# Mamba blocks in a four-layer kernel: the residual added by TensorE, softplus's correction on ScalarE and GpSimd, the layer norm's affine folded into weights

## The chip, the cores and the metric

The kernel runs on one core of a Trainium2 chip. The metric is the device time of one execution in microseconds, the median of several runs. All arithmetic is fp32.

## The reference, cut to what matters

Four layers follow each other on a tensor of 4 images, 96 channels, 64 x 64 pixels. Layers 0 and 2 are two Mamba blocks with a fusion and a batch norm, layer 1 is another state-space layer (ssd), layer 3 a ConvNeXt block. The change touches layers 0 and 2 only. One Mamba block, with L = 4096 positions, C = 96, DIN = 192, 16 states:

```python
mu = seq.mean(-1, keepdims=True)
var = ((seq - mu) ** 2).mean(-1, keepdims=True)
h = (seq - mu) * jax.lax.rsqrt(var + EPS) * ln_g + ln_b
xz = h @ in_w
xs, z = jnp.split(xz, 2, axis=-1)
xp = jnp.pad(xs, ((0, 0), (DCONV - 1, 0), (0, 0)))
xc = sum((conv_w[:, k] * xp[:, k:k + L, :] for k in range(DCONV))) + conv_b
xc = jax.nn.silu(xc)
dbl = xc @ xproj_w                      # dt, B, C
delta = jax.nn.softplus(dt @ dt_w + dt_b)
dA = jnp.exp(delta[..., None] * A)
dBx = delta[..., None] * Bm[:, :, None, :] * xc[..., None]
hstates = jax.lax.associative_scan(comb, (dA, dBx), axis=1)[1]
y = jnp.einsum('blds,bls->bld', hstates, Cm) + Dp * xc
y = y * jax.nn.silu(z)
return y @ out_w                        # and: seq = seq + this
```

## The kernel before, in words

**Stages.** `program` runs `mamba_fusion`, `ssd`, `mamba_fusion`, `convnext` one after the other. A Mamba stage keeps the whole sequence X of the four images in SBUF (96 partitions). It walks over 32 steps: 2 pairs of images, 2 blocks, 8 chunks of T = 512 positions. With two images of 192 channels a step has 384 channel rows, held as three tiles of 128 rows (j = 0, 1, 2).

**A step's two halves.** `mamba_front` prepares a step: layer norm (matmuls with `center` and `mean`, rsqrt on ScalarE), the input projection and the convolution as matmuls with tap-wise weights that already hold the convolution's factors (`wt["conv"]`), Silu, the projection to dt, B and C, softplus, and the products du = delta * xc. It is a generator; each `yield` is a place where the other half may go on. `Scan.run` walks over 24 groups of a step (3 tiles j, 4 quarters q, 2 halves). A group covers two times 128 rows, each 8 channels by 16 states, and 512 positions. The code of `run` issues, for group n: loads of delta rows four groups ahead, `decay` (the exponentials) two ahead, `spread` one ahead, the scan, `sums` two behind, `close` and `project` three and four behind, and as many pieces of the next step's `mamba_front` as the list `PACE` says.

**Who does what in a group.** Delta is written to DRAM (`dd`) and comes back by DMA spread over the states (`da`, a pool of 6 buffers). In three of four groups TensorE spreads du into PSUM (`bs`, L313, two buffers), VectorE multiplies it by B (L335), ScalarE turns da into decays in place (L107). In each fourth group (`dma`) ScalarE writes the decays into that PSUM tile (bs<-da), du comes by DMA (`dg`), and GpSimd multiplies by B (L308). VectorE scans (two instructions, L340), GpSimd multiplies the states by C (hc, L342; 3 buffers), ScalarE saves the last column (L345), TensorE sums over the states (py, L361). When a tile j is done, VectorE gates it (L369), TensorE projects it (po, L377), and VectorE adds it to X (L381).

**Softplus** is worked out as max(x, 0) + ln(1 + u) plus a correction, u = exp(-|x|): Abs, Exp, Ln on ScalarE, the maximum and first sum on VectorE (L267), w = u + 1 on ScalarE written over x in PSUM (L268), u - (w - 1) on VectorE (L270), the sum on GpSimd (L271), and then du (L248).

**Order.** A framework puts in the semaphores and also reorders: instructions are placed per engine by priority and readiness, so the order on an engine isn't quite that of the code. Each engine then works through its own order. The tile pools set how far one engine can be ahead: a tile name or tag with one buffer has to be read out before it is written again. `ua` and `lg` have one buffer each in the kernel before, PSUM's `mm` tag two.

**Activation tables.** Exp and Ln are wanted from one combined table set; `Tables` loads it once and again after each Silu or Gelu (L119), and keeps the exponentials behind a load by a dependency. If an instruction needs a function that the loaded set lacks, the build puts a load ahead of it; such a load carries the line of that instruction (L107).

Of the kernel before, what the change touches and what calls it, by code (L numbers as in the profile page):

```python
# [18 lines left out]
F32 = mybir.dt.float32  # L19
AF = mybir.ActivationFunctionType  # L20
ALU = mybir.AluOpType
# [4 lines left out]
B, C, HH, WW = 4, 96, 64, 64  # L26
L = HH * WW
P = 128
T = 512
# [6 lines left out]
DIN = 192  # L36
# [40 lines left out]
class Consts:  # L77
    def __init__(self, tc, pool):
        nc = tc.nc
        self.act = Tables(tc)  # L80
        self.norms = [pool.tile([C, 2], F32, name=f"bn{i}") for i in range(2)]
        self.ident = pool.tile([P, P], F32, name="ident")
        make_identity(nc, self.ident)

        self.center = pool.tile([C, C], F32, name="center")
        nc.vector.tensor_scalar(self.center, self.ident[:C, :C], -1.0 / C, None, ALU.add)
        self.mean = pool.tile([C, C], F32, name="mean")
        nc.vector.memset(self.mean, 1.0 / C)
        self.eps = pool.tile([P, 1], F32, name="eps")
        nc.vector.memset(self.eps, EPS)  # L90


class Tables:
# [29 lines left out]
def rsqrt(act, out, in_, eps):  # L123

    act.exp_ln(out, in_, AF.Ln, bias=eps)
    act.exp_ln(out, out, AF.Exp, scale=-0.5)
# [28 lines left out]
def mamba_front(tc, k, X, pools, wt, pair, c, h, made):  # L155

    nc = tc.nc  # L160
    work, psum, dram = pools
    if c == 0:
        nc.vector.memset(h[:C, :, 0:3], 0.0)
    else:
        nc.scalar.copy(h[:C, :, 0:3], h[:C, :, T : T + 3])

    def bank(name):
        return psum.tile([P, T], F32, tag="mm", name=name)

    for b in range(2):  # L170
        pc = bank("pc")[:C]
        nc.tensor.matmul(
            pc, lhsT=k.center, rhs=X[:, 2 * pair + b, ds(c * T, T)], start=True, stop=True
        )
        sq = work.tile([P, T], F32, tag="ua", name="sq")[:C]
        nc.scalar.activation(sq, pc, AF.Square)
        yield
        pv = bank("pv")[:C]
        nc.tensor.matmul(pv, lhsT=k.mean, rhs=sq, start=True, stop=True)
        rs = work.tile([P, T], F32, tag="lg", name="rs")[:C]  # L180
        rsqrt(k.act, rs, pv, k.eps[:C])
        yield
        dst = h[:C, b, 3 : 3 + T]
        nc.vector.tensor_tensor(dst, pc, rs, ALU.mult)
        nc.gpsimd.tensor_scalar(dst, dst, wt["ln"][:, 0:1], wt["ln"][:, 1:2], ALU.mult, ALU.add)


    xz = made["xz"] = work.tile([P, 6, T], F32, name="xz", bufs=2)
    for j in range(3):
        pu = bank("pu")  # L190
        for tap in range(4):
            kk = C + 1 if tap == 3 else C
            for r0, r1, d0, d1, b in SEGS[j]:
                nc.tensor.matmul(  # L194
                    pu[r0:r1], lhsT=wt["conv"][:kk, tap, d0:d1], rhs=h[:kk, b, ds(tap, T)],
                    start=(tap == 0), stop=(tap == 3),
                )
            yield
        nc.scalar.copy(xz[:, j], pu)
    k.act.other(xz[:, :3], xz[:, :3], AF.Silu)  # L200
    for j in range(3):
        pz = bank("pz")
        for r0, r1, d0, d1, b in SEGS[j]:
            nc.tensor.matmul(
                pz[r0:r1], lhsT=wt["in"][:, DIN + d0 : DIN + d1], rhs=h[:C, b, 3 : 3 + T],
                start=True, stop=True,
            )
        yield
        nc.scalar.copy(xz[:, 3 + j], pz)


    dbl = work.tile([P, T], F32, name="dbl")
    pd = bank("pd")
    for n in range(2):
        for b in range(2):
            j, r0, r1 = ROWS[b][n if b == 0 else 1 - n]
            nc.tensor.matmul(
                pd[2 * QUART * b : 2 * QUART * (b + 1)], lhsT=wt["xproj"][r0:r1, j],
                rhs=xz[r0:r1, j], start=(n == 0), stop=(n == 1),
            )  # L220
    yield
    nc.scalar.activation(dbl, pd, AF.Identity, bias=wt["one"])


    rows = dram.tile([P, T], F32, name="rows")
    nc.sync.dma_start(rows, dbl)
    bc = made["bc"] = work.tile([P, 2, 2, T], F32, name="bc", bufs=2)


    du = made["du"] = work.tile([P, 3, T], F32, name="du", bufs=2)  # L230
    for j in range(3):
        pt = bank("pt")
        for r0, r1, d0, d1, b in SEGS[j]:
            half = ds(HALFP * b, HALFP)
            nc.tensor.matmul(
                pt[r0:r1], lhsT=wt["dt"][half, d0:d1], rhs=dbl[half], start=True, stop=True,
            )
        delta = work.tile([P, T], F32, name="delta", bufs=2)
        softplus(nc, k.act, work, delta, pt)
        yield  # L240
        if j == 0:
            for b in range(2):
                for q in range(2):
                    r = HALFP * b + (QUART if q else RANK + 1)
                    nc.sync.dma_start(
                        bc[:, b, q], rows[r : r + NST, None].to_broadcast([NST, HEIGHT, T])
                    )
        nc.gpsimd.tensor_tensor(du[:, j], delta, xz[:, j], ALU.mult)  # L248
        for name, x in (("dd", delta), ("dg", du[:, j])):
            made[name, j] = dram.tile([P, T], F32, name=f"{name}{j}")  # L250
            nc.sync.dma_start(made[name, j], x)
    k.act.other(xz[:, 3:], xz[:, 3:], AF.Silu)
# [4 lines left out]
LEAD = 4  # L257


def softplus(nc, act, work, out, x):  # L260

    u = work.tile([P, T], F32, tag="ua", name="ua")
    t = work.tile([P, T], F32, tag="lg", name="lg")
    nc.scalar.activation(u, x, AF.Abs)
    act.exp_ln(u, u, AF.Exp, scale=-1.0)
    act.exp_ln(t, u, AF.Ln, bias=1.0)
    nc.vector.scalar_tensor_tensor(out, x, 0.0, t, ALU.max, ALU.add)  # L267
    nc.scalar.activation(x, u, AF.Identity, bias=1.0)  # L268

    nc.vector.scalar_tensor_tensor(t, x, 1.0, u, ALU.subtract, ALU.subtract, reverse1=True)  # L270
    nc.gpsimd.tensor_tensor(out, out, t, ALU.add)  # L271


class Scan:
# [96 lines left out]
    def project(self, g, b):  # L371

        nc = self.tc.nc
        xz, wt = g["made"]["xz"], g["wt"]
        po = self.psum.tile([P, T], F32, tag="po", name="po", bufs=1)[:C]
        for n, (j, r0, r1) in enumerate(ROWS[b]):
            nc.tensor.matmul(  # L377
                po, lhsT=wt["out"][r0:r1, j], rhs=xz[r0:r1, j], start=(n == 0), stop=(n == 1)
            )
        xs = self.X[:, 2 * g["pair"] + b, ds(g["c"] * T, T)]  # L380
        nc.vector.tensor_tensor(xs, xs, po, ALU.add)  # L381

    def run(self, steps, wts, front, first):

# [35 lines left out]
                next(ahead, None)  # L420


def mamba_weights(nc, act, ident, wpool, w, sub, one7):
    wt = {"one": one7}

    def load(name, shape):
        wt[name] = wpool.tile(shape, F32, name=f"w_{name}{sub}")
        nc.sync.dma_start(wt[name], w[name][sub])

    load("ln", [C, 2])  # L430
    load("in", [C, 2 * DIN])
    conv = wt["conv"] = wpool.tile([C + 1, 4, DIN], F32, name=f"w_conv{sub}")
    nc.sync.dma_start(conv[:C], w["conv_wT"][sub].partition_broadcast(C))
    nc.sync.dma_start(conv[C : C + 1, 3], w["conv_b"][sub : sub + 1])
    nc.vector.tensor_tensor(
        conv[:C], conv[:C], wt["in"][:, None, :DIN].to_broadcast([C, 4, DIN]), ALU.mult
    )
    xp = wt["xproj"] = wpool.tile([P, 3, 2 * QUART], F32, name=f"w_xproj{sub}")
    nc.vector.memset(xp, 0.0)
    nb = RANK + 1 + NST  # L440
# [26 lines left out]
def mamba_fusion(ctx: ExitStack, tc, k, src, dst, w):  # L467

    nc = tc.nc
    one = ctx.enter_context(tc.tile_pool(name="m1", bufs=1))  # L470
# [3 lines left out]
    work = ctx.enter_context(tc.tile_pool(name="mwork", bufs=1))  # L474
    state = ctx.enter_context(tc.tile_pool(name="mstate", bufs=3))
    psum = ctx.enter_context(tc.tile_pool(name="mps", bufs=2, space=PSUM))
    dram = ctx.enter_context(tc.tile_pool(name="mdram", bufs=3, space=DRAM))

    one7 = one.tile([P, 1], F32, name="one7")
    nc.gpsimd.memset(one7, 0.0)  # L480
    for q in range(0, P // QUART, 2):
        nc.gpsimd.affine_select(
            out=one7, in_=one7, compare_op=ALU.not_equal, fill=1.0, base=-(QUART * q + RANK),
            pattern=[[0, 1]], channel_multiplier=1,
        )
    h = one.tile([C + 1, 2, T + 3], F32, name="h")
# [8 lines left out]
    for b in range(2):  # L495
        nc.gpsimd.affine_select(
            out=sel["du"], in_=sel["du"], compare_op=ALU.not_equal, fill=1.0, base=-HALFP * b,
# [14 lines left out]
        nc.vector.bn_stats(stats[:, b * NT + c], xs)  # L512
        nc.sync.dma_start(dst[b, :, ds(c * T, T)], xs)

    wts = [mamba_weights(nc, k.act, k.ident, one, w, 0, one7)]
    carry = one.tile([P, 3, P // HEIGHT], F32, name="carry")
    steps = [(pair, sub, c) for pair in range(B // 2) for sub in range(2) for c in range(NT)]

# [10 lines left out]
    for n, _ in enumerate(front(0, made)):  # L529
        if n % 4 == 3 and n // 4 - 1 in range(B):  # L530
            b = n // 4 - 1
            nc.vector.reduce_sum(gsum[:, b : b + 1], X[:, b], axis=AX.X)
    wts.append(mamba_weights(nc, k.act, k.ident, one, w, 1, one7))

    gpw = one.tile([C, C], F32, name="gpw")
    nc.sync.dma_start(gpw, w["gp_wT"])
# [752 lines left out]
```

## Time and profile before

The median of three runs is 10016.03 us (10013.18 to 10017.02). The profiled execution has a span of 10008.9 us.

| stretch | us | TensorE | VectorE | ScalarE | GpSimd | clock | DMA share |
|---|---|---|---|---|---|---|---|
| Mamba 1, 500 to 592 us | 92 | 81.79 | 86.16 | 57.15 | 78.97 | 0.94 | 0.73 |
| Mamba 1, 1500 to 1592 us | 92 | 82.25 | 86.44 | 56.59 | 79.57 | 0.96 | 0.74 |
| ssd, 3060 to 6260 us | 3200 | 2759.58 | 2088.13 | 1538.09 | 1692.26 | 0.94 | 0.26 |
| Mamba 2, 7000 to 8000 us | 1000 | 871.57 | 935.20 | 625.66 | 852.01 | 0.96 | 0.73 |
| ConvNeXt, 9400 to 10008 us | 608 | 521.13 | 484.68 | 262.57 | 174.93 | 0.90 | 0.34 |

The columns are microseconds of busy time in the stretch; the clock is what TensorE was granted, as a share of full speed. In a line of the groups the columns are: source line, engine, operation, output <- inputs, shapes and count, then busy us, mean ns of one, and after the bar the idle time ahead of them with what ended most of it. A line of the waits gives who waited for whom, us in total, times, and the longest. A line of the timeline gives start us, duration us, engine, line, operation, and in brackets an idle time ahead of it. DVE is VectorE, ACT ScalarE, POOL GpSimd, PE TensorE.

### The profile page before, as it was taken

To read this page: it belongs to the slowest core of one execution; us is meant where nothing else is said; L and a number is where in the kernel's file an instruction comes from. 1 tells how busy PE (TensorE), PEld (TensorE's weight loads), DVE (VectorE), ACT (ScalarE), POOL (GpSimd) and SP (SyncE) were. 2 spreads that over 40 slices of the span, in tenths; PEclk is the share of its full clock that TensorE was granted. 3 is DMA by queue.
4 is the path that set the end of the run, shared out by engine and by line. 5 is a ranking of instruction groups with operands and counts; after the bars stand their busy time and mean duration, and the time that the engine had idled before them with its cause. 6 is when DMAs were issued, how large, how long until landed. Compare 5 with 4: busy or idle time off the path is not lost. (4 is left out here: it accounts for less than half of the span.)

```text
span 10008.9 us, 110272 instructions
## 1 busy us (share of the span) xinstructions
PE 8562.4 (86%) x33120; PEld 3566.0 (36%) x33120; DVE 8200.6 (82%) x10877; ACT 5497.9 (55%) x10460; POOL 6966.5 (70%) x4600
## 2 busy tenths in 40 slices
PE   7888888888886888888888888788888888887688
PEld 1222212222214766666776676122222222221122
DVE  7999999999994666667666666799999999999787
ACT  5566666656653445445445444566666665665244
POOL 6888888888883555555555555688888888888322
PEclk9999999999997999999999999899999999999798
DMA  7777777777773223223222221777777767777442
GB/s 190 200 205 204 201 206 207 201 201 209 204 197 105 72 66 94 65 66 95 72 66 74 81 64 51 188 201 204 210 200 203 208 196 204 207 204 199 113 99 73
DMA packets 802257, 1527.53 MB, mean 153 GB/s; under 512 B 123933, under 2 KB 127161, under 8 KB 800890
## 3 DMA queue, kind: packets, MB, share of 16 engines
q1 hardware_dynamic: 801658, 1520.47, 54.6%
q8 instruction: 263, 4.31, 0.2%
q14 instruction: 336, 2.75, 0.1%
HBM read 1229.30 MB, written 155.98 MB: 138 GB/s over the span
## 5 line engine op out<-in xcount | busy, mean ns | idle before, releaser
L342 POOL TENSOR_TENSOR hc<-hs,bc 128x1024 f32<-128x1024 f32 x1536 | 3608.0, 2355 | 622.2 <-DVE hs L340 554.8
L340 DVE TENSOR_TENSOR_SCAN hs<-da,carry,bs 128x512 f32<-128x512 f32 x2016 | 2466.4, 1264 | 79.2 <-POOL du L308 1.0
L107 ACT ACTIVATE da<-da,w_a 128x512 f32<-128x512 f32 x2304 | 1616.5, 716 | 1268.5 <-DMA da<-dd 1218.7
L361 PE MATMUL py<-hc,selsum 128*32 128x512 f32 x6144 | 1801.4, 638 | 462.5 <-POOL hc L342 448.3
L313 PE MATMUL bs<-du,seldu 64*128 64x512 f32 x4608 | 1573.3, 676 | 204.2 <-DVE hs L340 194.5
L335 DVE TENSOR_TENSOR bs<-bs,bc 128x1024 f32<-128x1024 f32 x1152 | 1397.7, 1213 | 184.0 <-PE bs L313 181.6
L308 POOL TENSOR_TENSOR du<-du,bc 128x1024 f32<-128x1024 f32 x384 | 904.5, 2355 | 281.3 <-DMA du<-dg 160.5
L863 POOL TENSOR_TENSOR seg<-seg,cb 128x384 f32<-128x384 f32 x512 | 514.7, 1006 | 818.1 <-DVE cb L862 750.0
L361 PEld LDWEIGHTS py<-hc,selsum 128*32 128x32 f32 x6144 | 240.6, 110 | 1815.1 <-POOL hc L342 1118.2
L313 PEld LDWEIGHTS bs<-du,seldu 64*128 64x128 f32 x4608 | 446.0, 195 | 1196.2 <-DVE hs L340 852.1
L848 DVE TENSOR_SCALAR seg<-dr,dac 128x128 f32<-128x128 f32 x1536 | 660.4, 458 | 256.9 <-PE y L892 249.3
L194 PE MATMUL pu<-h,w_conv 96*128 96x512 f32 (+3 forms) x2048 | 834.6, 629 | 6.5 <-ACT rs L107 6.3
L340 DVE TENSOR_TENSOR_SCAN hs<-bs,carry,du 128x512 f32<-128x512 f32 x672 | 823.5, 1260 | 7.8 <-issue 5.0
L799 PE MATMUL front<-pk,sconv 128*128 128x512 f32 x1536 | 767.9, 609 | 9.2 <-ACT z L787 5.1
L915 ACT ACTIVATE y<-yz 128x192 f32<-128x192 f32 x512 | 186.0, 363 | 919.3 <-DVE yz L914 918.3
L867 POOL TENSOR_TENSOR xs<-pre,coef 128x576 f32<-128x576 f32 x512 | 598.3, 1175 | 56.2 <-ACT pre L112 31.5
L810 PE MATMUL front<-sconv,pk 128*128 128x192 f32 x3072 | 577.2, 330 | 45.3 <-DVE pre L815 36.0
L1152 DVE SCALAR_TENSOR_TENSOR acc<-pad,c_conv,acc 96x1024 f32<-96x1024 f32 x336 | 491.9, 1468 | 109.1 <-ACT acc L1143 58.0
L902 POOL TENSOR_TENSOR y<-y,xs 128x192 f32<-128x192 f32 x496 | 293.5, 592 | 412.8 <-DVE y L901 412.1
L345 ACT COPY carry<-hs 128x2 f32<-128x2 f32 x1344 | 250.7, 187 | 564.2 <-DVE hs L340 560.4
L107 ACT ACTIVATE bs<-da,w_a 128x512 f32<-128x512 f32 x768 | 522.0, 680 | 2.5 <-DMA da<-dd 0.7
L810 PEld LDWEIGHTS front<-sconv,pk 128*128 128x128 f32 x3072 | 497.4, 191 | 69.3 <-DVE pre L815 57.7
(191 smaller groups left out, 13881.2 us busy)
## 6 DMA issues: line engine op xcount, KB each, us to landing
da<-dd SPq DMA_DIRECT2D x3072, 256.0 KB
du<-dg SPq DMA_DIRECT2D x768, 256.0 KB
dr<-rows SPq DMA_DIRECT2D x256, 384.0 KB
bc<-rows SPq DMA_DIRECT2D x256, 256.0 KB
dd<-delta SPq DMA_DIRECT2D x192, 256.0 KB
dg<-du SPq DMA_DIRECT2D x192, 256.0 KB
pk<-xn SPq DMA_DIRECT2D x128, 384.0 KB
pk<-xn SPq DMA_DIRECT2D x128, 256.0 KB
```

The costliest lines, as they stand in the source:

```text
L107: self.last = self.scalar.activation(out, in_, func, **kw)
L194: nc.tensor.matmul(pu[r0:r1], lhsT=wt["conv"][:kk, tap, d0:d1], rhs=h[:kk, b, ds(tap, T)], start=(tap == 0), stop=(tap == 3),)
L308: nc.gpsimd.tensor_tensor(g["du"], g["du"], self.b_or_c(g, 0), ALU.mult)
L313: nc.tensor.matmul(g["bs"][:, i], lhsT=self.sel["du"][rows, g["half"], g["q"]], rhs=g["made"]["du"][rows, g["j"]], start=True, stop=True,)
L335: nc.vector.tensor_tensor(dbx, dbx, self.b_or_c(g, 0), ALU.mult)
L340: nc.vector.tensor_tensor_scan(hs[:, i], da[:, i], dbx[:, i], init, ALU.mult, ALU.add)
L342: nc.gpsimd.tensor_tensor(g["hc"], hs, self.b_or_c(g, 1), ALU.mult)
L361: nc.tensor.matmul(py[rows], lhsT=self.sel["sum"][:, g["q"]], rhs=g["hc"][:, i], start=(g["q"] == 0), stop=(g["q"] == NQU - 1),)
L799: nc.tensor.matmul(p, lhsT=self.conv[:, i, DI + q * DST : DI + (q + 1) * DST], rhs=pk[:, i, ds(c * T, T)], start=(i == 0), stop=(i == 2),)
L810: nc.tensor.matmul(p, lhsT=pk[:, i, ds(c * Q, Q)], rhs=self.conv[:, i, :DI], start=(i == 0), stop=(i == 2),)
L848: nc.vector.tensor_scalar(seg[:, h], g["pair"]["dr"][:, c % 2 * NH + h], made["dac"][:, n0 + h : n0 + h + 1], 0.0, ALU.subtract, ALU.min,)
L867: nc.gpsimd.tensor_tensor(xs, x.to_broadcast([P, 3, NH, HD]), coef.to_broadcast([P, 3, NH, HD]), ALU.mult)
```

## The change

It has three parts, all in the Mamba stages. The residual: TensorE adds X into the projection's PSUM by a matmul with the identity, and ScalarE copies the sum back to X, in place of VectorE's addition. Softplus: the correction is worked out by two ScalarE instructions (u + 1, then - 1, with a bias tile `minus`) and a GpSimd subtraction, in place of ScalarE's one and VectorE's one; ScalarE writes to `lg` and no longer to PSUM, and `ua` and `lg` get two buffers. Layer norm: its gain is multiplied into the weights of convolution and z, its shift becomes one more weight row against a row of ones in h, made at the start by small matmuls (`shift`), so that GpSimd's affine on h falls away. What it is for: to take work off VectorE, and the affine off GpSimd.

```diff
@@ mamba_front
-        nc.vector.memset(h[:C, :, 0:3], 0.0)
+        nc.vector.memset(h[:, :, 0:3], 0.0)
     else:
-        nc.scalar.copy(h[:C, :, 0:3], h[:C, :, T : T + 3])
+        nc.scalar.copy(h[:, :, 0:3], h[:, :, T : T + 3])
...
-        sq = work.tile([P, T], F32, tag="ua", name="sq")[:C]
+        sq = work.tile([P, T], F32, tag="ua", name="sq", bufs=2)[:C]
...
-        rs = work.tile([P, T], F32, tag="lg", name="rs")[:C]
+        rs = work.tile([P, T], F32, tag="lg", name="rs", bufs=2)[:C]
         rsqrt(k.act, rs, pv, k.eps[:C])
         yield
-        dst = h[:C, b, 3 : 3 + T]
-        nc.vector.tensor_tensor(dst, pc, rs, ALU.mult)
-        nc.gpsimd.tensor_scalar(dst, dst, wt["ln"][:, 0:1], wt["ln"][:, 1:2], ALU.mult, ALU.add)
+        nc.vector.tensor_tensor(h[:C, b, 3 : 3 + T], pc, rs, ALU.mult)
...
-                    pu[r0:r1], lhsT=wt["conv"][:kk, tap, d0:d1], rhs=h[:kk, b, ds(tap, T)],
+                    pu[r0:r1], lhsT=wt["conv"][:, tap, d0:d1], rhs=h[:, b, ds(tap, T)],
...
-                pz[r0:r1], lhsT=wt["in"][:, DIN + d0 : DIN + d1], rhs=h[:C, b, 3 : 3 + T],
+                pz[r0:r1], lhsT=wt["z"][:, d0:d1], rhs=h[:, b, 3 : 3 + T],
@@ softplus
-    u = work.tile([P, T], F32, tag="ua", name="ua")
-    t = work.tile([P, T], F32, tag="lg", name="lg")
+    u = work.tile([P, T], F32, tag="ua", name="ua", bufs=2)
+    t = work.tile([P, T], F32, tag="lg", name="lg", bufs=2)
     nc.scalar.activation(u, x, AF.Abs)
     act.exp_ln(u, u, AF.Exp, scale=-1.0)
     act.exp_ln(t, u, AF.Ln, bias=1.0)
     nc.vector.scalar_tensor_tensor(out, x, 0.0, t, ALU.max, ALU.add)
-    nc.scalar.activation(x, u, AF.Identity, bias=1.0)
-
-    nc.vector.scalar_tensor_tensor(t, x, 1.0, u, ALU.subtract, ALU.subtract, reverse1=True)
-    nc.gpsimd.tensor_tensor(out, out, t, ALU.add)
+
+    nc.scalar.activation(t, u, AF.Identity, bias=1.0)
+    nc.scalar.activation(t, t, AF.Identity, bias=minus)
+    nc.gpsimd.tensor_tensor(u, u, t, ALU.subtract)
+    nc.gpsimd.tensor_tensor(out, out, u, ALU.add)
@@ Scan.project
+        xs = self.X[:, 2 * g["pair"] + b, ds(g["c"] * T, T)]
+        nc.tensor.matmul(po, lhsT=self.k.ident[:C, :C], rhs=xs, start=True, stop=False)
         for n, (j, r0, r1) in enumerate(ROWS[b]):
             nc.tensor.matmul(
-                po, lhsT=wt["out"][r0:r1, j], rhs=xz[r0:r1, j], start=(n == 0), stop=(n == 1)
-            )
-        xs = self.X[:, 2 * g["pair"] + b, ds(g["c"] * T, T)]
-        nc.vector.tensor_tensor(xs, xs, po, ALU.add)
+                po, lhsT=wt["out"][r0:r1, j], rhs=xz[r0:r1, j], start=False, stop=(n == 1)
+            )
+        nc.scalar.copy(xs, po)
@@ mamba_weights
+    shift = wpool.tile([C, C + 1], F32, name="w_shift")
+    nc.vector.memset(shift, 0.0)
+    nc.vector.tensor_copy(shift[:, C:], wt["ln"][:, 1:2])
+    for n in range(0, 5, 2):
+        m = min(2, 5 - n)
+        ps = psum.tile([P, T], F32, tag="mm", name="ps")[: C + 1, : m * DIN]
+        nc.tensor.matmul(ps, lhsT=shift, rhs=both[:C, n : n + m], start=True, stop=True)
+        nc.scalar.copy(both[C:, n : n + m].rearrange("p k n -> p (k n)"), ps[C:])
+    nc.vector.tensor_tensor(conv[C:, 3], conv[C:, 3], wx[C:], ALU.add)
+    nc.vector.tensor_scalar_mul(both[:C], both[:C], wt["ln"][:, 0:1])
```

## The prediction, made before the changed kernel ran

> **What bounds the kernel now.** I read the page first (busy shares, 40 slices), then the waits of VectorE, then one Mamba step on each engine in order of time. The page's slices show four stretches: VectorE is nine tenths busy in the two Mamba stages (to about 3050 us, and about 6250 to 9330 us); the rest is not touched by the change.
>
> ```profile
> PE 8562.4 (86%) x33120; PEld 3566.0 (36%) x33120; DVE 8200.6 (82%) x10877; ACT 5497.9 (55%) x10460; POOL 6966.5 (70%) x4600
> L342 POOL TENSOR_TENSOR hc<-hs,bc 128x1024 f32<-128x1024 f32 x1536 | 3608.0, 2355 | 622.2 <-DVE hs L340 554.8
> L340 DVE TENSOR_TENSOR_SCAN hs<-da,carry,bs 128x512 f32<-128x512 f32 x2016 | 2466.4, 1264 | 79.2 <-POOL du L308 1.0
> ```
>
> hc runs 1536 times, so 768 groups a stage, 24 to a step, 32 steps a stage, 64 in all. A step takes about 92 us, in which (500 to 592 us by the windows) VectorE works 86.2, GpSimd 79.0, TensorE 81.8 and ScalarE 57.2 us. On average VectorE is the bound, and its own waits are few (100 to 2900 us, 30 steps):
>
> ```profile
> DVE bs L335 <- PE bs L313: 88.5, 72, 4.1
> DVE lg L270 <- ACT pt L268: 18.3, 30, 2.0
> DVE h L184 <- ACT rs L107: 14.1, 17, 1.4
> ```
>
> But that average hides one place, the softplus stretch, where ScalarE sets the pace. I number the groups of a step 0 to 23; 1, 5, ... 21 are those whose decays ScalarE writes to PSUM (bs<-da), only one group ahead. Around group 17 the timeline of ScalarE reads:
>
> ```profile
> 597.07 0.71 ACT L107 ACTIVATE da<-da,w_a 128x512 f32<-128x512 f32 x1
> 598.81 0.62 ACT L107 ACTIVATE lg<-ua 128x512 f32<-128x512 f32 x1
> 600.12 1.28 ACT L112 ACT_TABLE_LOAD   x1
> 601.41 1.48 ACT L112 ACTIVATE xz<-xz 128x1536 f32<-128x1536 f32 x1
> 602.80 0.58 ACT L268 ACTIVATE pt<-ua 128x512 f32<-128x512 f32 x1
> 603.40 1.28 ACT L107 ACT_TABLE_LOAD   x1
> 604.70 0.69 ACT L107 ACTIVATE bs<-da,w_a 128x512 f32<-128x512 f32 x1
> ```
>
> and VectorE's:
>
> ```profile
> 605.48 2.46 DVE L340 TENSOR_TENSOR_SCAN hs<-bs,carry,du 128x512 f32<-128x512 f32 x2
> ...
> 622.81 1.20 DVE L335 TENSOR_TENSOR bs<-bs,bc 128x1024 f32<-128x1024 f32 x1
> ```
>
> Scan 17 starts 0.1 us after the last bs<-da ends (605.39), and 5.36 us after Silu's table load began. In six other steps that I looked at the distance is 5.36 to 5.45 too: scan 17 is fed just in time. The L107 table load (62 in the program, about one a step) is there because an exponential precedes the load that brings the combined set back (L119).
>
> **What the Trainium skill says.** "ScalarE: Activation LUTs", What ACT_TABLE_LOAD costs: 1283 ns, and a drain of about 1380 ns on top. The trace agrees on 1283 ns; the drain doesn't show, since the next instruction starts 1.30 us after the load. I take 1.30. The same page, Table sets: one set holds both exp and ln, and abs and identity are in every set. So Abs and Identity need no load, but Exp and Ln that alternate outside the combined set load each time. "PSUM — Partial Sum Buffer", Engine vs sequencer instructions: the queues of ScalarE, VectorE and GpSimd are strict FIFO. The trace agrees (the delta add, L271, waits behind hc), and so the built order decides what stands behind a late instruction. "GPSIMD Engine Reference", Engine selection: a two-input elementwise operation is about twice as slow as on VectorE. Here 1.27 us (L271) against 0.68 us (L270).
>
> **The change, part by part,** per step. Distances from start to start, since neighbours overlap by some 0.08 us.
>
> Residual: two X adds leave VectorE. They cost 0.58 to 0.60 us, but 0.39 where they fill the gap between a multiply (L335) and its scan: about 1.0 us. ScalarE gains two copies (0.5 each), TensorE two identity matmuls of some 1.1 us (records of 0.53, two per fp32 matmul); TensorE has 10 us of slack a step.
>
> Softplus: three corrections (L270) leave VectorE, 0.73 + 0.61 + 0.58 = 1.9 us, with a wait of 18.3/30 = 0.6 us. ScalarE gains three Identities (0.55 each), GpSimd three subtractions (1.3 each). Layer norm: two affines of 0.77 us leave GpSimd, and with them part of the wait of h and of the multiply after it (1.28 + 0.54 us in this step). The three weight matmuls, the ScalarE copies and two VectorE operations stand before the first pc: about 5 us a stage, taken from the first matmuls' 2.02 us each.
>
> Were VectorE the only limit, this would be 1.0 + 1.9 + 0.6 + some 1.2 = 4.7 us a step, 300 us. GpSimd would come to 79.0 + 3.9 - 1.5 = 81.4, under VectorE.
>
> Table loads: the built program's order on ScalarE tells another story. With two buffers for ua and lg the softplus instructions of several j move forward past Silu. In 54 of the 64 steps the stretch now stands: da, Abs, da, Exp, load, Silu, **load**, Ln, carry, Abs, **load**, bs<-da, Identity, Exp, Identity, **load**, Ln, **load**, bs<-da, ... **load**, Ln, load. The L107 loads go from 62 to 278: 216 more, 4 in each of 54 steps, 277 us of ScalarE. It has 35 us idle a step, but not here. From the first da (597.07) to scan 17, before: 8.4 us. After, with the same durations: da .61, Abs .52, da .61, Exp .52, load 1.29, Silu 1.39, load 1.30, Ln .52, carry .09, Abs .52, load 1.30, bs .63, Identity .55, Exp .52, Identity .55, load 1.30, Ln .52, load 1.30, bs .69, hand-over .1 = 14.8 us. It can't start earlier: that da needs a DMA into a buffer (6 of them) that scan 14 frees, and it lands some 3.5 us later. So scan 17 comes 6.4 us later. Behind the last bs<-da nothing on VectorE can pass; before it VectorE has nothing left to do but two maxima (L266).
>
> GpSimd's burst: the new order there is hc17, three softplus operations, du (L308), hc18, three operations, hc19; before it was a pair, hc17, hc18, du, hc19. And on TensorE the matmul that feeds the multiply of group 22 stands behind the sum of hc19 (and one po). Counted from the start of scan 17: scan 2.4, hc 2.35, three 3.9, du 2.3, hc 2.35, three 3.9, hc 2.35, three matmul pairs 3.15, hand-overs .3 = 23.0 us. Before: 622.81 - 605.48 = 17.3 (19.8 in the step at 1069 us). VectorE alone, with the removed work gone, would need 16.9, so some 6 us of it is a new wait, <-PE bs and behind it <-POOL hc. Then multiply, h, scan 22, multiply and scan 23, multiply: 8.9 us to scan 24, so 31.9 us from scan 17 to scan 24, against 29.1 before (28.1 and 28.8 in two others): +2.8.
>
> Sum of such a step: +6.4 + 2.8 - 0.4 (the X add outside the stretch) = +8.8 us; 54 x 8.8 = 475. In the other steps, first and boundary ones, bs<-da comes before Silu and only GpSimd's burst remains: about +2 x 8 = 16. Weights 2 x 5 = 10. 10016 + 475 + 16 + 10 = 10517; I say 10515.
>
> **The rivals.** *The loads are hidden and VectorE's relief counts:* about 62 x 4.7 = 290 us less, 9725. For it speak 86.2 of 92 us busy and ScalarE's 55%; against it scan 17, which already starts 0.1 us after ScalarE. 6%. *ScalarE's block delays, but GpSimd's burst is absorbed* (waits that overlap, another order of hand-overs): then scan 17 to 24 takes 26.0 us instead of 29.1; +6.4 - 3.1 - 0.4 = +2.9 a step, 10016 + 54 x 2.9 + 10 = 10183. For it speaks that VectorE waits 0.9 us in all on hc now; against it the order. 15%. *Delay and relief cancel:* within 0.2%, 3%. *More:* stores of delta and du stand ahead of the next da loads in the DMA queue's new order, so loads wait for GpSimd's bursts; or a throttled clock doubles those three pairs: +12 a step, 10690. 8%. Both delays as worked out: 68%.
>
> **How the numbers follow.** Forecast 10515. The drain of 1.38 us, were it real for the four extra loads, would add 5.5 us a step (10810); the trace shows none, and I leave that out. The range, 10230 to 10620, takes the main case with 5 us less to 2 us more a step, and the upper part of the absorbed one. Faster 0.06, same 0.03, slower 0.91.
>
> **What would show it.** L107 (then L109) table loads at 278. In a step, five of them between two Silu loads, and scan 17 starting about 12.5 us after Silu's load instead of 5.4. VectorE waits on ScalarE (delta or hs <-ACT) of 5 to 7 us a step, new. VectorE waits <-PE bs of some 5 us after scan 21. VectorE busy about 215 us less while the span grows. Were scan 17 on time, or the multiply of group 22 not waiting, that step of my sum would be wrong; were the exps spread over idle ScalarE time, the kernel would be faster.

## The result, and the profile after

The changed kernel takes 10662.8 us (median, 10647.2 to 10669.3); the kernel before took 10016.5 us on the same chip. The ratio is 1.064, with a 95% interval of 1.0621 to 1.0658: 646 us slower. The forecast was 10515, with a range that ended at 10620. The direction was right, the size too small.

The page after, busy times and two groups:

```profile
PE 8884.1 (83%) x33400; PEld 3636.2 (34%) x33400; DVE 8055.7 (76%) x10574; ACT 5964.4 (56%) x11008; POOL 7115.1 (67%) x4664
L342 POOL TENSOR_TENSOR hc<-hs,bc 128x1024 f32<-128x1024 f32 x1536 | 3605.2, 2357 | 827.6 <-DVE hs L340 759.3
L340 DVE TENSOR_TENSOR_SCAN hs<-da,carry,bs 128x512 f32<-128x512 f32 x2016 | 2469.4, 1266 | 100.5 <-DVE bs L335 1.9
```

VectorE lost work as the change meant it to: the additions of X and the corrections lasted 216 us together; as neighbours overlap, its busy time fell by 145 (8200.6 to 8055.7 us), where the prediction said about 215. Its share went from 82% to 76%. The two operations shown cost what they did; TensorE's matmuls got longer (L361, py: 638 to 662 ns on average). ScalarE gained 467 us, of which 277 are table loads; their group, by line and engine:

```profile
L109 ACT ACT_TABLE_LOAD x278 | 356.7, 1283 | 4.9
```

The waits of VectorE from 100 to 3000 us (a line: who waited for whom, us, times, longest), after:

```profile
DVE bs L335 <- PE bs L313: 248.5, 91, 8.4
DVE delta L266 <- ACT lg L109: 143.6, 45, 5.5
DVE stats L528 <- ACT X L527: 31.8, 23, 3.1
DVE hs L340 <- POOL du L247: 27.4, 20, 1.4
```

Before, in this stretch, the first was 92.0 us and the second 2.7 (L267); the last two were not among the largest. L527, in the third line, is not the residual's copy (L382) but the fusion's activation, which both kernels have; it waits in turn for the fusion's matmul:

```profile
ACT X L527 <- PE pf L526: 35.2, 11, 4.3
```

One affected step shows where they stand. ScalarE, in order of time:

```profile
558.51 1.28 ACT L114 ACT_TABLE_LOAD   x1
559.81 1.48 ACT L114 ACTIVATE xz<-xz 128x1536 f32<-128x1536 f32 x1
561.31 1.28 ACT L109 ACT_TABLE_LOAD   x1
562.60 0.63 ACT L109 ACTIVATE lg<-ua 128x512 f32<-128x512 f32 x1
...
563.83 1.28 ACT L109 ACT_TABLE_LOAD   x1
565.12 0.69 ACT L109 ACTIVATE bs<-da,w_a 128x512 f32<-128x512 f32 x1
...
567.51 1.28 ACT L109 ACT_TABLE_LOAD   x1
568.81 0.63 ACT L109 ACTIVATE lg<-ua 128x512 f32<-128x512 f32 x1
569.46 1.28 ACT L109 ACT_TABLE_LOAD   x1
570.75 0.69 ACT L109 ACTIVATE bs<-da,w_a 128x512 f32<-128x512 f32 x1
```

In this block each Ln and each bs<-da has a load of its own in front. VectorE in the same step:

```profile
569.47 0.69 DVE L266 SCALAR_TENSOR_TENSOR delta<-pt,lg 128x512 f32<-128x512 f32 x1 [5.51 <-ACT lg L109]
571.53 2.46 DVE L340 TENSOR_TENSOR_SCAN hs<-bs,carry,du 128x512 f32<-128x512 f32 x2 [1.37 <-POOL du L247]
...
594.26 1.23 DVE L335 TENSOR_TENSOR bs<-bs,bc 128x1024 f32<-128x1024 f32 x1 [5.81 <-PE bs L313]
```

571.53 is scan 17: 13.02 us after Silu's load, where it was 5.36. The multiply of group 22 follows 22.73 us later, where it was 17.3. GpSimd between the two, first before the change (there scan 17 starts at 605.48), then after:

```profile
608.09 4.69 POOL L342 TENSOR_TENSOR hc<-hs,bc 128x1024 f32<-128x1024 f32 x2
613.35 2.35 POOL L308 TENSOR_TENSOR du<-du,bc 128x1024 f32<-128x1024 f32 x1 [0.57 <-issue]
615.65 2.36 POOL L342 TENSOR_TENSOR hc<-hs,bc 128x1024 f32<-128x1024 f32 x1
...
574.13 2.35 POOL L342 TENSOR_TENSOR hc<-hs,bc 128x1024 f32<-128x1024 f32 x1 [2.61 <-DVE hs L340]
576.44 1.27 POOL L270 TENSOR_TENSOR ua<-ua,lg 128x512 f32<-128x512 f32 x1
577.79 1.27 POOL L271 TENSOR_TENSOR delta<-delta,ua 128x512 f32<-128x512 f32 x1
579.13 1.27 POOL L247 TENSOR_TENSOR du<-delta,xz 128x512 f32<-128x512 f32 x1
...
588.89 6.97 POOL L342 TENSOR_TENSOR hc<-hs,bc 128x1024 f32<-128x1024 f32 x3
```

The three softplus operations come a second time (584.97 to 588.93) ahead of 588.89, the hc of group 19. Before the change that hc (615.65) started 10.2 us after scan 17; now it starts 17.4 us after it.

In this step (block 0 of the first pair) that is all. In steps of the second pair the same multiply waits up to 8.45 us, and TensorE shows why. The sum behind that hc, and the matmuls that feed that multiply, first in this step, then in one of the second pair:

```profile
591.28 1.05 PE L361 MATMUL py<-hc,selsum 128*32 128x512 f32 x4 [1.28 <-POOL hc L342]
592.80 2.27 PE L313 MATMUL bs<-du,seldu 64*128 64x512 f32 x7
...
2043.32 3.97 PE L313 MATMUL bs<-du,seldu 64*128 64x512 f32 x7
```

The same seven records take 2.27 or 3.97 us. In the two Mamba windows 100 to 1500 and 1500 to 2900 us the granted clock fell from 0.95 and 0.96 to 0.90.

I cut the steps of the first 3000 us, from one z-Silu table load to the next, at scan 17 and scan 24, and took the means of 27 steps before and of 18 affected ones after. Steps at and beside a change of block are left out, since Silu stands elsewhere in them:

| piece of a step, us | before | after | change | forecast of the change |
|---|---|---|---|---|
| Silu's load to scan 17 | 5.4 | 13.0 | +7.6 | +7.1 |
| scan 17 to scan 24 | 28.9 | 32.8 | +3.9 | +2.8 |
| scan 24 to the next Silu's load | 58.5 | 58.3 | -0.2 | -1.1 |
| sum | 92.8 | 104.1 | +11.3 | +8.8 |

The forecast's third piece is what its sum left: X's addition gone (-0.4), and Silu's load 0.7 us sooner after the first da.

For the whole, I cut both stages of the two profiled executions, which are 10667.2 - 10008.9 = 658 us apart, from the first scan of a step to the first scan of the next. The 54 affected steps grew by 600 us, 11.1 each. The six steps at a change of block grew by 29, 4.8 each; the first step of the program by 14, that of the second Mamba stage by 3. The time ahead of the two stages' first scans, where the weights are made, grew by 14 (5 and 9, ssd included in the second). The last steps and the end give 3 back. That sums to 657.

### The profile page after: what moved, and what is told of

It is laid out like the page before. It is cut to its first block, busy times and chain, and to the rows that moved or that the text cites. A ratio compares the mean times of both kernels' runs of the same rounds, so it can differ in the third digit from the quotient of the medians.

```text
span 10667.2 us, 110712 instructions
## 1 busy us (share of the span) xinstructions
PE 8884.1 (83%) x33400; PEld 3636.2 (34%) x33400; DVE 8055.7 (76%) x10574; ACT 5964.4 (56%) x11008; POOL 7115.1 (67%) x4664
## 3 DMA queue, kind: packets, MB, share of 16 engines
q1 hardware_dynamic: 802106, 1520.47, 53.6%
## 5 line engine op out<-in xcount | busy, mean ns | idle before, releaser
L340 DVE TENSOR_TENSOR_SCAN hs<-da,carry,bs 128x512 f32<-128x512 f32 x2016 | 2469.4, 1266 | 100.5 <-DVE bs L335 1.9
L361 PE MATMUL py<-hc,selsum 128*32 128x512 f32 x6144 | 1880.9, 662 | 663.3 <-POOL hc L342 660.4
L109 ACT ACTIVATE da<-da,w_a 128x512 f32<-128x512 f32 x2304 | 1612.3, 717 | 1020.4 <-DMA da<-dd 910.0
L313 PE MATMUL bs<-du,seldu 64*128 64x512 f32 x4608 | 1599.3, 707 | 294.5 <-DVE hs L340 287.0
L335 DVE TENSOR_TENSOR bs<-bs,bc 128x1024 f32<-128x1024 f32 x1152 | 1396.8, 1213 | 540.3 <-PE bs L313 531.1
L361 PEld LDWEIGHTS py<-hc,selsum 128*32 128x32 f32 x6144 | 244.2, 112 | 2078.1 <-POOL hc L342 1296.4
L340 DVE TENSOR_TENSOR_SCAN hs<-bs,carry,du 128x512 f32<-128x512 f32 x672 | 822.1, 1261 | 78.6 <-POOL du L247 64.3
L193 PE MATMUL pu<-h,w_conv 97*64 97x512 f32 (+1 forms) x2048 | 840.2, 631 | 6.8 <-ACT rs L109 6.4
L109 ACT ACTIVATE bs<-da,w_a 128x512 f32<-128x512 f32 x768 | 522.7, 681 | 5.0 <-DVE hs L340 1.7
```

What stands on the lines that cost most here:

```text
L109: self.last = self.scalar.activation(out, in_, func, **kw)
L193: nc.tensor.matmul(pu[r0:r1], lhsT=wt["conv"][:, tap, d0:d1], rhs=h[:, b, ds(tap, T)], start=(tap == 0), stop=(tap == 3),)
L313: nc.tensor.matmul(g["bs"][:, i], lhsT=self.sel["du"][rows, g["half"], g["q"]], rhs=g["made"]["du"][rows, g["j"]], start=True, stop=True,)
L335: nc.vector.tensor_tensor(dbx, dbx, self.b_or_c(g, 0), ALU.mult)
L340: nc.vector.tensor_tensor_scan(hs[:, i], da[:, i], dbx[:, i], init, ALU.mult, ALU.add)
L361: nc.tensor.matmul(py[rows], lhsT=self.sel["sum"][:, g["q"]], rhs=g["hc"][:, i], start=(g["q"] == 0), stop=(g["q"] == NQU - 1),)
```

## The experiments

Two theories stood at first. *Loads:* the extra table loads in ScalarE's block ahead of scan 17 carry most of the loss. *Burst:* GpSimd's groups of three softplus operations, ahead of hc and the matmul behind it, carry what the loads don't. Two rivals: TensorE's lower clock with its identity matmuls, and X's copy on ScalarE, which delays those that read X (the fusion's matmul, and behind it bn_stats). All times below are medians; ratios are to the kernel before, run on the same chip.

| kernel | L109-type loads | us | ratio, 95% interval |
|---|---|---|---|
| after | 278 | 10662.8 | 1.0640, 1.0621 to 1.0658 |
| e1: after, Silu behind all exponentials | 0 | 10383.0 | 1.0353, 1.0337 to 1.0369 |
| e5: after, subtraction on VectorE | 230 | 10610.9 | 1.0582, 1.0566 to 1.0598 |
| e6: both | 0 | 10250.9 | 1.0219, 1.0201 to 1.0237 |
| e4: after, one buffer for ua and lg | 122 | 10745.4 | 1.072, 1.070 to 1.074 |
| e13: after without GpSimd's correction | 270 | 10371.6 | 1.0348, 1.0331 to 1.0366 |
| e12: e1 without GpSimd's correction | 0 | 10131.4 | 1.0108, 1.0087 to 1.0129 |
| e10: e1, residual on VectorE | 0 | 10341.3 | 1.0321, 1.0306 to 1.0337 |
| e3: residual and norm, softplus as before | 122 | 10253.7 | 1.0225, 1.021 to 1.024 |
| e8: e3, Silu behind all | 0 | 10118.9 | 1.0097, 1.0082 to 1.0112 |
| e14: norm alone | 62 | 10061.4 | 1.0034, 1.0021 to 1.0047 |
| e11: residual alone, Silu behind all | 0 | 10107.6 | 1.0082, 1.0066 to 1.0099 |
| e7: before, Silu behind all | 0 | 10119.0 | 1.0096, 1.0072 to 1.0119 |
| e16: before, Silu issued early | 0 | 10321.8 | 1.0300, 1.0277 to 1.0323 |
| e17: after, Silu issued early | 0 | 10356.5 | 1.0332, 1.0311 to 1.0353 |
| e18: e3, Silu issued early | 0 | 10123.4 | 1.0099, 1.0077 to 1.0121 |
| e20: e17 with 192 needless loads | 192 | 10465.4 | 1.0444, 1.0418 to 1.047 |

### The loads: e1, and the subtraction: e5, e6, and the buffers: e4

e1 changes only what the Silus may pass:

```diff
     def exp_ln(self, out, in_, func, **kw):
         self.last = self.scalar.activation(out, in_, func, **kw)
         self._behind(self.last, self.loaded)
+        self.since.append(self.last)
     def other(...):
         self._behind(ins, self.last)
+        for x in self.since:
+            self._behind(ins, x)
+        self.since = []
```

> The changed kernel, with one dependency more: a Silu stands behind every exponential and logarithm issued since the last table load, not behind the last one alone. In the built program the extra table loads fall from 278 to 0 (62 before the change); GpSimd's three operations a tile stay. Theory (table loads hold back scan 17, GpSimd's burst is the smaller part): scan 17 is on time, some 9 us a step come back, 10000 to 10150 us. Rival 1 (GpSimd's burst is the cause, the loads lie in idle ScalarE time): over 10350 us. Rival 2 (TensorE's lower granted clock, 0.96 to 0.90 in the Mamba stages, is a cause of its own, set by the extra matmuls): clock stays at 0.90 and the time over 10250 us.

1.0640 - 1.0353 = 2.9% of 10016 = 287 us less: about 5.3 us in each of 54 steps, and four loads last 5.2. The theory's 10000 to 10150 is missed, and the time lies where both rivals had it (over 10350; over 10250 with the clock still at 0.91). That 5.3 lies near 5.2 is no measure of a load: the edit also moves Silu, and the pieces of a step, further down, show that 287 us is what is left of a larger gain and a loss. What VectorE waits for in e1 (L340 is its multiply):

```profile
DVE bs L340 <- PE bs L318: 261.7, 129, 7.2
DVE delta L271 <- POOL du L252: 57.3, 22, 2.9
```

The wait for ScalarE's lg is gone (12.4 us are left of 143.6), the one behind TensorE is not.

e5 and e6 put `ua<-ua,lg` on VectorE, after and in e1:

```diff
-    nc.gpsimd.tensor_tensor(u, u, t, ALU.subtract)
+    nc.vector.tensor_tensor(u, u, t, ALU.subtract)
```

> The changed kernel with softplus's subtraction back on VectorE (two GpSimd operations a tile as before the change), table loads not mended: 230 of them, and all four extra ones ahead of scan 17 are still there. Theory: scan 17 stays late (about 13 us after Silu's load); only the chain behind it gets shorter, 22.7 to some 20.3 us, so 10480 to 10580 us. Rival 1 (GpSimd's burst): 10100 to 10250 us. Rival 2 (clock): no change, 10600 to 10700 us.

> Both edits: Silu behind all, and the subtraction on VectorE. No extra load, no burst. What is left of the change: residual on TensorE and ScalarE, layer norm's affine in the weights, two ScalarE Identities for one. Theory: a little faster than the kernel before, 9850 to 10000 us, for VectorE loses the two additions of X and waits less on ScalarE. Rival 2 (clock): over 10100 us.

They gain 0.6% and 1.3%, where the burst theory wanted more; 10611 and 10251 both lie in the clock rival's range. The timeline of e6, VectorE and GpSimd around one subtraction, shows what it cost instead:

```profile
540.51 2.35 POOL L347 TENSOR_TENSOR hc<-hs,bc 128x1024 f32<-128x1024 f32 x1 [1.82 <-DVE hs L345]
...
541.42 1.98 DVE L275 TENSOR_TENSOR ua<-ua,lg 128x512 f32<-128x512 f32 x1
543.33 0.68 DVE L271 SCALAR_TENSOR_TENSOR delta<-pt,lg 128x512 f32<-128x512 f32 x1
```

The subtraction takes 1.98 us, and ends 0.5 us after hc. The next one, with one input in PSUM, takes 0.68. The mean of the 192 subtractions is 1.648 us, 0.97 more, so VectorE has 186 us more work than 192 subtractions of 0.68 us would be (in e5 the mean is 0.902). e6 therefore doesn't measure GpSimd's part cleanly.

e4 takes the second buffer of ua and lg away (`bufs=2` struck out in four places):

> The changed kernel with one buffer for ua and lg, as before the change. In the built program 122 extra table loads instead of 278 (two a step, both ahead of scan 17), and GpSimd's three operations are spread wider apart. Theory: scan 17 comes 3 us later than before the change, and the chain behind it takes some 19 us instead of 22.7: 10100 to 10300 us. Rival 1 (burst alone, the amount of GpSimd work being the same): 10450 us and more. Rival 2 (clock): 10550 us and more.

Only 122 loads are left, and it is the slowest of all, as both rivals had it. The count of loads alone doesn't tell the time. Up to here the rivals fit the times better than the theories.

### GpSimd's burst: e13 and e12

In both, the correction's GpSimd operations are left out (delta lacks it), in the changed kernel and in e1:

```diff
-    nc.gpsimd.tensor_tensor(u, u, t, ALU.subtract)
-    nc.gpsimd.tensor_tensor(out, out, u, ALU.add)
```

> The changed kernel as it is, with softplus's two GpSimd operations left out, so that delta lacks the correction; the table loads stay (270 of 278). Prediction's steps: the way from scan 17 to scan 24 shrinks by 4 to 6 us a step, the 13.0 us from Silu's load to scan 17 stay: 10350 to 10450, and TensorE's half-speed matmuls ahead of the multiply of group 22 vanish with its idle time. Rival (GpSimd is not what the multiply waits for): above 10600.

> The changed kernel without extra table loads (10383 in its run), with softplus's two GpSimd operations left out, so that delta lacks the correction; both Identities stay on ScalarE. Burst theory: four operations of 1.27 us leave the chain from scan 17 to the multiply of group 22, 5.1 us a step and some of it given back to other waits: 10050 to 10160, about the kernel with residual and norm alone (10119). Rival (order on ScalarE, the Identities, the two buffers): above 10300.

Both came as the burst theory said: 2.9% (292 us, 5.4 a step over 54) and 2.45% (245 us). The waits of VectorE in e13, to set against those of after:

```profile
DVE delta L266 <- ACT lg L109: 159.8, 48, 5.5
DVE bs L333 <- PE bs L311: 148.8, 81, 6.2
```

The wait behind TensorE falls by 100 us in this stretch, the one for ScalarE stays, as does scan 17 at 13.0 us. Of 2000 instructions compared on each, table loads aside, 97% on ScalarE and over 99% on VectorE stand in the same order as in after, so little else moved. With loads and burst both out (e12) the loss is 1.1% instead of 6.4%.

The steps show the two apart. Means of 27 steps of the first stage (its first step, its last and those at a change of block left out), in us:

| kernel | scan 0 to scan 17 | scan 17 to the next scan 0 |
|---|---|---|
| before | 63.6 | 29.1 |
| after: loads and burst | 71.3 | 32.8 |
| e13: loads, no burst | 71.0 | 28.0 |
| e1: burst, no extra loads | 61.7 | 37.3 |
| e12: neither | 61.5 | 33.2 |
| e7: before, Silu behind all | 61.9 | 32.6 |

Without the extra loads scan 17 comes 9.6 us sooner with the burst and 9.5 without it, and what follows gets 4.5 to 5.2 us longer. Without the burst what follows gets 4.8 us shorter with the loads and 4.1 without them, and scan 17 stays within 0.4 us. So the two causes act in different places, and their effects nearly add up. The 9.5 us is more than four loads last (5.2): the edit of e1 also takes Silu and its load (2.8 us) from ahead of scan 17 to behind it, where that load starts 8 us after scan 17. The rest of the 9.5 is not traced.

One detail of the expectation failed: half-speed matmuls are fewer but not gone. In a step of the second pair the identity matmul and pv behind it still take 1.79 and 1.92 us for two records each, the seven records of bs 2.68 instead of 3.97.

### What is left over, and whether relief is worth anything: e7, e8, e10, e11, e14, e3

e7 is the kernel before with e1's edit, e11 adds the residual's edit to it, e8 the norm's as well. e10 is e1 with the residual put back:

```diff
-        nc.tensor.matmul(po, lhsT=self.k.ident[:C, :C], rhs=xs, start=True, stop=False)
...
-        nc.scalar.copy(xs, po)
+        nc.vector.tensor_tensor(xs, xs, po, ALU.add)
```

> The kernel before, with nothing changed but that each Silu stands behind every exponential issued since the last load: its 62 extra table loads fall away. Theory (a load ahead of scan 17 costs what it lasts, because scan 17 is fed by ScalarE just in time): 62 x 1.3 = 80 us less, 9920 to 9950. Rival (VectorE sets the end of the step, ScalarE's moment is only a touch): no change, 10000 to 10030.

> The change without its softplus part (softplus as before, one buffer each), no extra table loads. Burst theory (GpSimd's six extra operations in the softplus stretch are what is left over, 365 us above the kernel before, when the loads are gone): residual and norm alone do no harm, 9850 to 9950. Rival 1 (TensorE's identity matmuls and its lower clock, ScalarE's X copy ahead of bn_stats): at least half of the 365 stays, 10150 to 10350.

> The changed kernel with no extra table loads (10383 in the run before) and the residual again on VectorE. Burst theory: as without this edit, 10340 to 10420, the GpSimd work being the same. Rival 1 (identity matmuls, clock, X copy): 10100 to 10250, and TensorE's clock back near 0.94.

> The kernel before without extra loads, with the residual's identity matmul and ScalarE copy alone; norm and softplus as before. Burst theory: VectorE loses 1.0 us of work a step, so 9860 to 9940. Rival 1: 10080 to 10250, with waits of bn_stats on the X copy and a clock lower by some 0.03.

e7 contradicts both of its expectations: 62 loads fewer, and 1% slower. Holding Silu back until every exponential is through has a price of its own; in e7 VectorE waits 163.1 us for bs<-PE, against 92.0 in the same stretch before. The table above has its place: scan 17 comes 1.7 us sooner, and 3.5 us more pass behind it. So e1's 287 us are a saving net of such a price, and e12's remaining 1.1% is no more than what e7 pays without any part of the change. Between e7, e11 and e8 there is no difference beyond the intervals: residual and norm, at the same order rule, neither help nor harm. (e11's 10108 lies in its rival's range and e8's 10119 a little below it, but e7 stands there without any residual.) e10, as the burst theory had it, is 0.3% under e1, with intervals that touch, so beside the new softplus the residual on TensorE and ScalarE costs little or nothing. bn_stats waits 0.4 us for the fusion in e10 and 42.4 in e1 (100 to 3000 us), so that wait is worth no more than this either. So the identity matmuls and X's copy are left with 0.3%. Nor do the identity matmuls lower the clock: it is 0.91 in e10 and in e1, and in e11 (0.94) no lower than in e7 (0.93). The clock as such is not tested apart; e3, below, is 2.2% slower than the kernel before at the same 0.94.

e14 and e3 keep the table loads where the build puts them; e14 has the norm's fold alone, e3 the residual as well.

> The kernel before with the norm's affine folded into the weights and nothing else (62 extra loads, as before). If GpSimd's affine stands in the way of h and of the multiply behind it: 1.0 to 1.5 us a step less, 9930 to 9980. If another wait ends there instead: within 20 us of the kernel before.

> The change without its softplus part, table loads as the build places them: 122 instead of 62, two a step. If a load ahead of scan 17 costs what it lasts and the residual nothing else: 60 x 1.3 = 80 us more than the norm alone, 10020 to 10080. If the X copy and the identity matmuls cost on top: 10120 to 10200. If the second load is hidden: below the norm alone.

The norm alone is 0.34% slower, although GpSimd's affine is gone; both of e14's expectations are missed. The residual then adds 1.9% (191 us), with 60 more loads: 3.2 us for each, more than a load lasts, and above all of e3's ranges. The loss lies in ScalarE's block: in e3 scan 17 starts 10.3 us after Silu's load (median of the 27 steps) instead of 5.4 in e14, and scan 0 to scan 17 takes 68.9 us instead of 63.8, while scan 17 to the next scan 0 takes 28.4 instead of 29.5. So here too an edit that takes VectorE work away changed what stands ahead of scan 17.

### Silu issued early, and a dose of loads: e16, e17, e18, e20

In e16 to e18 one line moves. The Silu of z stood behind softplus in the code, but was ready long before and so slipped between its instructions; now it is issued ahead of them:

```diff
         nc.scalar.copy(xz[:, 3 + j], pz)
+    k.act.other(xz[:, 3:], xz[:, 3:], AF.Silu)
...
-    k.act.other(xz[:, 3:], xz[:, 3:], AF.Silu)     # end of mamba_front
```

> The kernel before with one line moved: the Silu of z is issued right behind z's copies from PSUM, ahead of softplus, so no exponential can slip between it and its reload (0 extra loads instead of 62) and it waits for none of softplus's. Theory (ScalarE's block of load, Silu, load ahead of scan 17 sets that stretch): 2 to 4 us a step less, 9760 to 9900. Rival (VectorE or the multiply's matmul ends there anyway, as it did with Silu put behind the exponentials): 9990 to 10120.

> The changed kernel with the same line moved (0 extra loads instead of 278). If the loads cost what they last, as with Silu held back (10383), and the order costs 100 there (it cost 100 on the kernel before): 10250 to 10300, GpSimd's burst being left. If GpSimd's three-operation groups spread out once ScalarE hands them over evenly: 10000 to 10150. If the order on ScalarE costs nothing: 10360 to 10400.

> Residual and norm with softplus as before, the Silu of z moved forward, 0 extra loads instead of 122 (10254 with them). If it is the loads' order that made the residual cost 190 us there: 9750 to 9950, below the kernel before. If the X copy and the identity matmuls cost: 10050 to 10200.

e16 was expected to beat the kernel before. It is 3% slower, above both of its ranges: with ScalarE out of the way, VectorE waits for other things (xz<-PE py, 84.6 us in 2900; du from GpSimd, 39.5). e17 stands at e1's time within 27 us though its order is another one, and in none of its ranges (10360 to 10400, no cost of the order, is the nearest). VectorE waits for GpSimd in another place; its largest wait there:

```profile
DVE hs L340 <- POOL du L308: 225.1, 53, 7.1
```

The scan of a group with du by DMA now waits 7.1 us for its multiply on GpSimd, which stands behind softplus's operations. e18 is 2% under e16: with this order the residual and the norm are worth 200 us, with the other two they were worth nothing or cost. It is still 1% above the kernel before, in the range given for a cost of X's copy and the identity matmuls.

e20 was meant to dose loads alone. It is e17 with a needless load of the set that is already there, ahead of each Ln:

```diff
     act.exp_ln(u, u, AF.Exp, scale=-1.0)
+    act.again()        # preload_act_table_set(EXP_LN), behind the last exponential
     act.exp_ln(t, u, AF.Ln, bias=1.0)
```

> The changed kernel with the Silu of z moved forward, and one needless load of the combined set ahead of each Ln of softplus: 192 loads that do nothing, three a step, order of all else kept. If a load in that stretch costs what it lasts: 192 x 1.3 = 250 us more than the kernel with the line moved alone. If it is hidden beside other engines: under 60 more. If it costs more than itself, through TensorE's clock and GpSimd: over 350 more.

192 loads, each 1283 ns on ScalarE, and 1.1% or 109 to 112 us more; that lies between the expectations. It is not the price of a load, because the order of all else was not kept. In the step around 550 us ScalarE does the Exp of two tiles in a row and then both Ln in e17; in e20 the first Ln comes ahead of the second Abs, and the Identity of one tile stands between the Abs and the Exp of the next. Scan 17 comes 19.5 us after Silu's load instead of 9.9 (means of 27 steps), and scan 17 to the next scan 0 takes 28.6 us instead of 35.1. So e20 says no more than that loads and order move together here.

In the changed kernel's block the timeline shows scan 17 just behind the last bs<-da. That the four loads cost their full 1.30 us there is read from that chain; no run takes them out of the block with all else in place, so it isn't shown apart.

## Why the prediction was right in direction and too small

What failed is the size of four terms of the sum, not the path. Scan 17 was to come 6.4 us later and comes 7.0 later; the way from it to scan 24 was to grow by 2.8 us and grew by 3.9; the rest of a step was to shrink by 1.1 and shrank by 0.2, since VectorE's saving was counted and the wait that takes its place put at nothing; the other eight steps were to cost 2 us each and cost 29 + 14 + 3 = 46 together.

**Table loads (right in mechanism, some 0.6 us short).** 278 loads, five between two Silu loads, and the wait of VectorE for ScalarE of 5.5 us stood where the order on ScalarE had them. The block from its first da to scan 17 was forecast at 14.8 us and took 15.37 (556.16 to 571.53): scan 17 comes 7.0 us later instead of 6.4. The term was mis-sized by some 0.6 us, and the trace shows where: a load starts 0.02 us after the end of the instruction ahead of it, while other neighbours on ScalarE overlap by about 0.1 us. From start to start, Exp ahead of a load takes 0.63 us instead of 0.52, Silu 1.50 instead of 1.39, Abs 0.61 instead of 0.52, Ln 0.65 instead of 0.52, the second Identity (L269) 0.72 instead of 0.55: 0.6 us together. The prediction took the distances without a load behind. The Trainium skill, "ScalarE: Activation LUTs", What ACT_TABLE_LOAD costs, speaks of a drain of about 1380 ns on top. The changed kernel shows none either: behind each of the 278 loads the next instruction starts 1.29 to 1.30 us after the load's start. Leaving it out was right.

**GpSimd's burst (right in mechanism, one size off).** The forecast had the multiply of group 22 at 23.0 us after scan 17; it stood at 22.73, and scan 24 at 31.8 against 31.9, in the step shown. Its contrast to the absorbed case, 31.9 - 26.0 = 5.9 us a step, is what e13 took away: 5.4. In the mean of the 18 steps it is not that close: the multiply stands 23.6 us after scan 17, scan 24 another 9.2 after it (forecast 8.9), and before the change the whole way took 28.9 on average, not 29.1. That makes +3.9 instead of +2.8, and 0.6 of the 1.1 us lies ahead of the multiply. There the three matmul pairs were priced at full speed, 3.15 us. In many later steps they run at half speed, and scan 24 comes up to 34.5 us after scan 17. The prediction had named this under *More* ("a throttled clock doubles those three pairs") and given it 8%. Its other cause there, loads late behind stores in the DMA queue, isn't what happened: ScalarE's waits for da<-dd fell from 585.2 to 381.5 us (100 to 3000 us). The Trainium skill, "TensorE: Matmul & The Clock Gate", What's actually happening, says that an idle array is throttled and activity releases it. The trace fits: in the step of 2043.32 TensorE waits 4.30 us for hc (2034.23), its records from there on take twice the time, and so do those that feed the multiply. In the step shown first it waits 4.15 us (585.06) and is slow too (1.92 and 2.02 us), but is back at full speed in time. Slow pairs occur before the change as well (2.02 us at 1081.41, behind a wait of 2.61), so the half speed could have been put into the main case. No run kept TensorE busy to test it.

**VectorE's relief (wrong in most steps).** The step "- 0.4 (the X add outside the stretch)", with Silu's load 0.7 us sooner, was to shorten the third piece by 1.1 us; it shortened by 0.2. VectorE did work less there, 53.6 instead of 55.2 us (means of 20 steps), but its waits for the matmul that spreads du (bs L335 <- PE bs) grew from 2.0 to 3.0 us. The saving came through in one of the four blocks (58.5 to 57.2 us, block 0 of the second pair); in the first pair's block with statistics the piece grew from 58.5 to 60.0, with 3.6 us of that wait instead of 1.9. The wait of bn_stats has no part in this: nearly all of it lies between scan 17 and scan 24. That the relief is worth nothing by itself is what e7, e11 and e8 show, which lie together; e18 and e16 show that with another order it can be worth 200 us.

**Other steps (too low).** They were to cost 2 us each. The six at a change of block took 4.8, and the program's first step 14.

**Sum.** Between the two profiled executions 658 us came where the sum had 501. Of the 157 us missed, 600 - 475 = 125 lie in the affected steps, 46 - 16 = 30 in the other eight; the weights' 10 us were about right (14 with all that stands ahead of the first scans). The mechanism stands, and the terms were each too small. The range ended at 2 us a step above the main case, 10620; the affected steps alone were 2.3 off. Half speed was held to be a rival instead of a part of each step's spread.

The other rivals fell: *loads hidden* (9725) and *absorbed* (10183), the last because e13, in which the burst is gone, is 292 us faster.

What stays open: why Silu held back costs 1% on the kernel before, and Silu issued early 3%. The steps show where the time is (scan 17 to the next scan 0 takes 32.6 and 32.8 us instead of 29.1), not a rule by which it could have been foreseen. How the loads' loss divides between the loads themselves and the order around them is open too. No version here beats the kernel before.

## What to carry to other kernels

Before moving work off the busiest engine, look at what feeds it in the stretch concerned, and compare the built order on the engines that gain the work: here two ScalarE buffers more let instructions of different table sets interleave, and a burst on GpSimd stood ahead of what TensorE and VectorE waited for. VectorE's busy share told nothing of what its relief was worth here: a saving counts only where no wait takes its place. Price a chain through TensorE behind an idle stretch at half speed as well as at full. And after an edit that is to test one thing, compare the built order again: e20's had moved.

## What was not expected of the hardware

VectorE's subtraction with both inputs in SBUF took 1.98 and 1.91 us in e6 beside GpSimd's hc, on average 1.648 us, and the addition with one input in PSUM 0.68. The Trainium skill, "GPSIMD Engine Reference", Specifications, has the SBUF interfaces shared with VectorE, with contention for VectorE's instructions with two SBUF inputs. The traces agree: in e6 the one shown ends half a microsecond after hc does, and in e5 the 58 of the same subtractions that met GpSimd idle took 0.69 us on average, the 86 that lay beside its instructions for more than half of their time 1.18, and up to 2.77. So reading one operand from PSUM, as the kernel before did in its correction, would save 1 us an instruction on average in e6 and 0.2 in e5 (mean 0.902), and nothing where GpSimd is idle.

The lost overlap in front of a table load, 0.1 us each time, was not expected either.
